# A message-passing graph layer on one core: single-row fetches four a step on two queues, edge loads one group at a time, and the pipeline's lags taken in at the fiftieth group from the end

## The chip, the core and the metric

The kernel runs on one core of a Trainium2 chip. Its engines are TensorE (PE; its weight loads are shown apart as PEld), VectorE (DVE), ScalarE (ACT), GpSimd (POOL) and SyncE (SP). SP computes nothing here: it loads registers and issues transfers. ACT and POOL issue transfers too, beside their other work. The metric is the device time of one execution in microseconds (us), lower is better.

## What is computed

The reference is one layer of a graph network over 12,500 nodes of 64 features and 200,000 edges, sorted by destination node, followed by a residual and a layer norm. Shortened to what matters (`ssp` is softplus minus ln 2):

```python
nodes = x[[src, dst]]                            # 200000 x 128, gathered rows
gates = ssp(edge_state @ We1 + be1) @ We2 + be2
gates = gates * (1 - sigmoid(5 * (distance - 3.5)))
h = ssp(nodes @ Wn1 + bn1) @ Wn2 + bn2
messages = h * gates
message_sum = zeros.at[dst].add(messages)        # scatter-add
new_state = x + (ssp(message_sum @ Ws1 + bs1) @ Ws2 + bs2)
out = layernorm(x + new_state)
```

## The kernel before, in words

**Tiling.** The edges are cut into 391 groups of 512 (`NG`), each held as four slots (`K = 4`) of 128 edges. The rows of `x` for an edge's source must be fetched one by one. The destination side needs no gather: a table of `x @ Wn1` (lower half) is made in a preparation of about 75 us, and since edges are sorted, the destinations of 256 edges lie within 42 consecutive nodes (`W`), so `load` (line 231) brings a strip of 42 table rows per half group.

**How source rows come.** A slot is normally filled by one indirect gather on POOL (`gather`, line 193, issued in line 205): 128 rows of 256 bytes, indices in `src_i`. Some slots are instead filled row by row with ordinary 256-byte transfers by SP's and ACT's queues (`fetch`, line 209, issued in line 225 after the row numbers were put in registers by the load of line 218). SP fills 14 slots at 5 rows a step, ACT 17 slots at 6 rows a step (`SYNC_ROWS`, `SCALAR_ROWS`, `slots_by_rows`, line 102); these slots lie in tiles `xr`, the gathered ones in `xg`. 18 `xg` buffers exist (`AHEAD + BEHIND`), and a gather is issued 14 groups ahead.

**A step.** The main loop (line 592) runs over steps `i`. Its order is written out by hand and the engines keep it. In a step before `ends = 390 - CATCH_UP`, SP issues the loads of group `i+5` (line 236 the edge features `eT`, in even steps for two groups at once; line 240 loads registers; line 245 twice the table strip `wns`), then its rows. PE does for different groups: the edge half of the second layer of group `i-1` (lines 303, 307), the first layer of group `i+1` (270, 272, 278), the scatter by a one-hot matrix of group `i-3` (330), the transposes of group `i+3` (261) and the node half of the second layer of `i-1` (313). ACT does the exponential of group `i+1` (line 289), two single rows, the logarithm (292), two rows, the copy of the transposed rows of `i+3` (266) and two rows. DVE does the softplus' last part (297), products (322, 326), the sum into `sums` (347) and the one-hots of group `i+5` (251). So three lags stand between the transposes of a group, its first layer, its second layer and its scatter.

**Waits that order the queues.** The loads of group `g` are kept behind the scatter of group `g - 11` (`old`, line 232). The first instruction of PE's step (line 303) takes the waits of the step upon itself: the loads of the group, and the gather and the one-hots of the group to be transposed (`needs`, line 600).

**The end.** From step `ends` on, another branch (line 631) is run, in which the lags shrink: second layer lag 1 to 0, scatter lag 3 to 1, transposes from `i+3` to `i+1`; the order on PE is transposes, first layer, second layer, scatter. `CATCH_UP = 10` makes this 10 steps from the last group.

**Node blocks.** Whenever 512 more nodes are complete, their output is made by a chain of parts (`node_block`, line 349) strewn over the following steps: 25 blocks, whose PE work is in lines 366, 394 and 397, with one load and one store on SP each.

The lines that set the rates of rows and the order within a step:

```python
fetch(i, nc.sync)
...
at(exps, i + 1)
fetch(i, nc.scalar, 0, 3)
at(logs, i + 1)
fetch(i, nc.scalar, 1, 3)
for g in ahead[i]:
    transposes(g)
    xcopy(g)
fetch(i, nc.scalar, 2, 3)
```

Of the kernel before, what the change touches and what calls it, by code (L numbers as in the profile page):

```python
# [32 lines left out]

# [3 lines left out]

# [5 lines left out]
F32 = mybir.dt.float32  # L43
BF16 = mybir.dt.bfloat16
I32 = mybir.dt.int32
# [11 lines left out]
P = 128  # L57
D = 64
HE = 256
# [6 lines left out]
AHEAD = 14  # L66
LOADS = 5
SPREADS = 5
CATCH_UP = 10
PREPARE = 5  # L70
FREE = 5
BEHIND = 4


BLOCK_STEPS = ((2, 3, 4, 4, 6, 7, 8, 9, 10, 14), (2, 3, 3, 4, 5, 6, 7, 8, 9, 10), (1, 2, 1, 2, 3))
SYNC_ROWS = 5
SCALAR_ROWS = 6
CUTOFF = 5.0
EPS = 1e-5
LN2 = 0.6931471805599453  # L80
# [18 lines left out]
    return steps  # L99


def slots_by_rows(NG, k, rows):

    ready = [-(-(n + 1) * P // rows) + 6 for n in range(NG)]
    return [(g, k) for g in ready if g < NG - 2]


@with_exitstack
def gnn_resnorm_kernel(ctx: ExitStack, tc: tile.TileContext, a: dict, out: bass.AP, E: int):
# [63 lines left out]
    def note(key, ins):  # L173
        made.setdefault(key, []).append(ins)
        return ins

    def behind(ins, *keys):

        for key in keys:
            for other in made.get(key, []):  # L180
                tc.add_manual_dep(ins.ins, other.ins.name,
                                  mybir.DependencyInfo(mybir.DependencyClass.Sync, mybir.DependencyReason.DATA),
                                  reason="one place of a step takes its waits")

    lists, by_rows = {}, []
    for engine, name, k, rows in ((nc.sync, "rows_sync", K - 1, SYNC_ROWS), (nc.scalar, "rows_scalar", K - 2, SCALAR_ROWS)):
        lists[engine] = rows, slots_by_rows(NG, k, rows), const.tile(a[name].shape, I32, name=name)
        by_rows += lists[engine][1]

    def padding(g, k):  # L190
        return g * GE + k % 2 * HE + k // 2 * P >= E
# [14 lines left out]
                out=xg[:, k, :D], out_offset=None, in_=x,  # L206
                in_offset=bass.IndirectOffsetOnAxis(ap=src_i[:, g, k : k + 1], axis=0)))

    def fetch(i, engine, part=0, parts=1):

        rows, slots, rows_i = lists[engine]
        at = i * rows
        total = min(rows, len(slots) * P - at)
        if i < 0 or total <= 0:
            return
        if part == 0:
            n, first = divmod(at, rows_i.shape[1])
            _, row_at[engine] = nc.values_load_multi_w_load_instructions(  # L218
                rows_i[n : n + 1, first : first + total], engines=[engine.engine], min_val=0, max_val=N - 1,
                skip_runtime_bounds_check_because="src holds rows of x")  # L220
        for j in range(part * rows // parts, min(total, (part + 1) * rows // parts)):
            n, r = divmod(at + j, P)
            if r == 0:
                xrs[slots[n]] = loads.tile([P, P], F32, name=f"xr{slots[n][1]}", bufs=2)
            note(("gather", slots[n][0]), engine.dma_start(xrs[slots[n]][r : r + 1, :D],  # L225
                                                           x[bass.ds(row_at[engine][j], 1), :]))

    row_at = {}
    bases = {}

    def load(g):
        old = ("scatter", g - LOADS - 2 - 4)
        if g % 2 == 0:
            n = min(2, NG - g)
            both = loads.tile([P, 2, HE], F32, name="eT", bufs=4)
            behind(note(("load", g), nc.sync.dma_start(both[:, :n], a["eT"][:, g : g + n, :])), old)
            for j in range(n):
                eTs[g + j] = both[:, j]
        if g % 2 == 0:
            _, at = nc.values_load_multi_w_load_instructions(  # L240
                base_i[0:1, 2 * g : 2 * g + 4], engines=[SP], min_val=0, max_val=N - 1,
                skip_runtime_bounds_check_because="they were clamped to these bounds")
            bases[g], bases[g + 1] = at[:2], at[2:]
        for h in range(2):
            behind(note(("load", g), nc.sync.dma_start(wns[D:DW, g % REST, h, :], table[bass.ds(bases[g][h], W), :])),  # L245
                   old)
# [39 lines left out]
    def exps(g, part=every):  # L286
        if part.start == 0:
            us[g] = work.tile([P, 3 * HE], F32, name="u")
        nc.scalar.activation(us[g][:, part], z_of(g)[:, part], AF.Exp)  # L289
# [147 lines left out]
    with tc.manual_schedule():  # L437
# [4 lines left out]
        with tc.tile_pool(name="prep", bufs=1) as prep:  # L442
# [10 lines left out]

            for i in range(3):
                load_x(i)
            nc.sync.dma_start(lists[nc.sync][2], a["rows_sync"])
            nc.sync.dma_start(lists[nc.scalar][2], a["rows_scalar"])
            dist = cut.rearrange("p g k -> p (g k)")
            nc.sync.dma_start(dist, a["dist_l"])
            dst_i = rel.bitcast(I32)  # L460
# [106 lines left out]
        with tc.tile_pool(name="finish", bufs=1) as finish:  # L567
# [24 lines left out]
            for i in range(-3, last - 1):  # L592
                now = parts.pop(i, [])
                early = [part for part in now if part.tensor]
                at(load, i + LOADS)
                fetch(i, nc.sync)
                if i >= 0:
                    at(gather, i + AHEAD, i < BEHIND)
                if i < ends:
                    needs = [("xcopy", i + 1), ("load", i + 1)]  # L600
                    needs += [(name, g) for g in ahead[i] for name in ("gather", "onehot")]
                    for g in second[i]:
                        layer2_edge(g, *needs)
                    if i >= -1:
                        zs[i + 1] = z_tile()
                        layer1_edge(i + 1)
                        for part in early:
                            part.tensor(tx_tile())
                    if i >= -1:
                        layer1_node(i + 1)  # L610
                    for n, g in enumerate(third[i]):
                        scatter(g, zs[i + 1][:, 1, HE + 2 * W * n : HE + 2 * W * (n + 1)])
                    at(exps, i + 1)
                    fetch(i, nc.scalar, 0, 3)
                    at(logs, i + 1)
                    fetch(i, nc.scalar, 1, 3)
                    for g in ahead[i]:
                        transposes(g)
                        xcopy(g)
                    fetch(i, nc.scalar, 2, 3)  # L620
                    for g in second[i]:
                        layer2_node(g)
                    for g in second[i]:
                        hcut(g)
                        message(g)
                    for g in third[i]:
                        window(g)
                    for part in early:
                        part.others()
                    at(softplus, i + 1)  # L630
                else:
# [3 lines that stand above are left out]
                    zs[i + 1] = z_tile()  # L635
                    layer1_edge(i + 1)
                    for part in early:
                        part.tensor(zs[i + 1][:, 1, HE:])
                    layer1_node(i + 1)
                    exps(i + 1)  # L640
                    logs(i + 1)
                    for g in second[i]:
                        layer2(g)
                        hcut(g)
                        message(g)
                    softplus(i + 1)
                    for g in third[i]:
                        scatter(g, tx_tile()[:, : 2 * W])
                        window(g)
                    for part in early:  # L650
                        part.others()
                for g in ahead[i]:
                    at(onehot, g + 2)
                for part in now:
                    if not part.tensor:
                        part.others()
                complete = third[i][-1] + 1 if third[i] else 0
                if blocks and complete >= blocks[0][1] - PREPARE and not begun:
                    begun = node_block(*blocks[0][0], finish)
                    begun.pop(0).others()  # L660
                if blocks and complete >= blocks[0][1]:
                    steps = next(steps for steps in BLOCK_STEPS if i + steps[-1] < last - 1)
                    for n, part in zip(steps, begun):
                        parts.setdefault(i + n, []).append(part)
                    rest = begun[len(steps) :]
                    blocks.pop(0)
                    begun = None
# [119 lines left out]
def layouts(inputs):  # L787
# [18 lines left out]

    out = {"x": np.ascontiguousarray(x)}
    out["src_l"] = lanes(src, 0)
    for name, k, rows in (("rows_sync", K - 1, SYNC_ROWS), ("rows_scalar", K - 2, SCALAR_ROWS)):
        v = out["src_l"].reshape(P, NG, K)[(slice(None), *zip(*slots_by_rows(NG, k, rows)))].T.reshape(-1)  # L810
        n = lcm(P, rows)
        out[name] = padded(v, -(-v.shape[0] // n) * n, 0).reshape(-1, n)
    out["dst_l"] = lanes(dst, dst[-1])
    out["dist_l"] = lanes(dist, 1e6)
    out["dst_h"] = np.ascontiguousarray(padded(dst, NR * P * HE, dst[-1]).reshape(NR, P, HE).transpose(1, 0, 2))
# [42 lines left out]
```

## Time and profile before

| | |
|---|---|
| Time, median of 3 runs | 2429.64 us (2419.54 to 2435.27) |
| Time of the profiled execution | 2429.64 us |
| Span of the profiled execution, first to last instruction | 2427.7 us |
| Granted TensorE clock, mean over the span | 0.870 |
| Busy: PE, PEld | 2099.0 us (86%), 1723.6 us (71%) |
| Busy: POOL, DVE, ACT | 1453.4 us (60%), 1068.8 us (44%), 941.2 us (39%) |
| Mean rate of the DMA engines | 59 GB/s |

The profile is one execution as the hardware profiler saw it, on a page with several views: busy time by engine, the span in 40 slices, the queues, the chain of work that ended last (followed back from the last instruction, at each step to what released it), the costliest groups of instructions by source line, and the issued transfers. Engine names with a q (SPq, ACTq) are the engine's instruction queue, which issues transfers and loads registers; that is not counted as busy. In a line of the view of waits stand the engine and line that waited, what ended the wait, the total in us, how often, and the longest. A busy PE is not PE at full speed: when the granted clock is low its instructions take longer.

### The profile page before, as it was taken

Reading aid. Unit: us, or ns where it says so; the run is one execution under the profiler, and the core shown is the slowest. Engines: PE = TensorE matmul, PEld = TensorE weight load, DVE = VectorE, ACT = ScalarE, POOL = GpSimd, SP = SyncE. Lnnn points to the kernel's source line nnn. Section 1 sums busy time; section 2 is a strip of 40 time slices with the busy share of each in tenths; the row PEclk is TensorE's granted clock in tenths of the full one; section 3 lists DMA queues with packets and bytes.
Section 4 is the critical chain, followed back from the end, with each engine's and each line's share of the span. In section 5 each row is a group of like instructions: output and inputs, shape, how many; then the busy total and the mean of one; then the engine's idle time right before and its main releaser. Section 6 shows DMA issues by size and latency. Waiting matters only on the chain.

```text
span 2427.7 us, 48622 instructions
## 1 busy us (share of the span) xinstructions
PE 2099.0 (86%) x11373; PEld 1723.6 (71%) x11373; DVE 1068.8 (44%) x2763; ACT 941.2 (39%) x1318; POOL 1453.4 (60%) x1536
## 2 busy tenths in 40 slices
PE   5889888888788888988888888888988888888997
PEld 5777776766667676776777777777777777777775
DVE  4344333433344344343434444444444444444564
ACT  1334333433334334333434334444444444443453
POOL 6767555655657556555656656666566666665630
PEclk9989777987899779688878888999899898898997
DMA  7322212221222122122222222222222222222220
GB/s 226 102 60 61 50 45 50 55 51 43 53 51 62 46 48 58 43 53 53 58 48 57 51 55 57 56 63 59 54 60 60 57 57 59 56 64 54 60 61 8
DMA packets 147206, 143.55 MB, mean 59 GB/s; under 512 B 47912, under 2 KB 94426, under 8 KB 146916
## 3 DMA queue, kind: packets, MB, share of 16 engines
q1 hardware_dynamic: 92172, 88.01, 12.8%
q0 software_dynamic: 49024, 50.30, 10.7%
q10 hardware_dynamic: 5720, 2.07, 0.4%
q8 instruction: 97, 1.59, 0.3%
q14 instruction: 193, 1.58, 0.2%
HBM read 130.58 MB, written 9.63 MB: 58 GB/s over the span
## 4 chain that ended last, share of the span: by engine, by line
PE 46%; SPq 21%; DMA 10%; issue 10%; ACTq 7%; ACT 5%; DVE 1%; DVEq 0%
PE z L278 11%; SPq L218 7%; PE z L272 7%; PE gh L307 7%; DMA xr<-in_x 6%; ACTq L225 5%; SPq L245 5%; PE z L330 5%; PE gh L313 5%; SPq L225 4%; PE gh L303 3%; ACT xT L266 3%; PE tx L261 3%; DMA wns<-table 3%; SPq L240 3%
## 5 line engine op out<-in xcount | busy, mean ns | idle before, releaser
L205 POOL DMA_INDIRECT xg<-in_x,src_i x1532 | 1453.2, 949 | 883.3 <-PE z L330 398.5
L297 DVE SCALAR_TENSOR_TENSOR s<-u,z 128x768 f32<-128x768 f32 x392 | 372.9, 951 | 709.0 <-ACT u L292 698.8
L292 ACT ACTIVATE u<-u,one 128x768 f32<-128x768 f32 x392 | 365.9, 934 | 781.0 <-DMA xr<-in_x 771.1
L278 PE MATMUL z<-xT,wns 106*128 106x256 f32 x1564 | 494.2, 447 | 0.0
L289 ACT ACTIVATE u<-z 128x768 f32<-128x768 f32 x392 | 316.3, 807 | 398.1 <-PE z L330 122.1
L313 PE MATMUL gh<-consts,s 128*128 128x64 f32 x3128 | 423.9, 282 | 0.0
L313 PEld LDWEIGHTS gh<-consts,s 128*128 128x128 f32 x3128 | 419.0, 208 | 0.0
L278 PEld LDWEIGHTS z<-xT,wns 106*128 106x128 f32 x1564 | 351.2, 226 | 64.0 <-ACT xT L266 0.7
L303 PE MATMUL gh<-row,ones 3*128 3x512 bf16 x391 | 157.5, 403 | 258.2 <-ACT xT L266 232.7
L322 DVE TENSOR_TENSOR h<-gh,cut 128x256 f32<-128x256 f32 x391 | 164.8, 421 | 347.2 <-PE gh L313 340.5
L272 PE MATMUL z<-eT,consts 128*128 128x256 f32 x782 | 314.7, 488 | 0.0
L307 PE MATMUL gh<-consts,s 128*128 128x128 f32 x1564 | 307.3, 324 | 0.0
L330 PEld LDWEIGHTS z<-xg,msg 128*128 128x128 f32 x1512 | 277.8, 229 | 33.3
L266 ACT COPY xT<-tx 106x512 f32<-106x512 f32 x391 | 225.2, 576 | 186.6 <-DMA xr<-in_x 134.6
L307 PEld LDWEIGHTS gh<-consts,s 128*128 128x128 f32 x1564 | 226.0, 208 | 99.5 <-issue 98.9
L261 PE MATMUL tx<-consts,xg 128*106 128x128 f32 x1533 | 272.9, 306 | 27.3 <-ACT xT L266 23.2
L330 PE MATMUL z<-xg,msg 128*128 128x84 f32 x1512 | 256.3, 300 | 0.0
L347 DVE TENSOR_TENSOR sums<-sums,z 64x42 f32 x756 | 148.7, 197 | 234.0 <-ACT u L289 159.9
L303 PEld LDWEIGHTS <-ones 3*128 3x128 bf16 x391 | 35.7, 91 | 298.2 <-ACT xT L266 258.9
L261 PEld LDWEIGHTS tx<-consts,xg 128*106 128x106 f32 x1533 | 210.6, 161 | 31.9 <-ACT xT L266 26.7
L326 DVE TENSOR_TENSOR msg<-gh,h 128x256 f32<-128x256 f32 x391 | 166.0, 424 | 13.4
L272 PEld LDWEIGHTS z<-eT,consts 128*128 128x128 f32 x782 | 131.9, 212 | 54.1 <-issue 15.4
(101 smaller groups left out, 716.7 us busy)
## 6 DMA issues: line engine op xcount, KB each, us to landing
eT<-in_eT SPq DMA_DIRECT2D x195, 256.0 KB
xr<-in_x ACTq DMA_DIRECT2D x2176, 0.2 KB
xr<-in_x SPq DMA_DIRECT2D x1792, 0.2 KB
xg<-in_x,src_i POOLq DMA_INDIRECT x1532
wns<-table SPq DMA_DIRECT2D x782, 21.0 KB
table<-tb SPq DMA_DIRECT2D x14, 448.0 KB
sums<-in_xT SPq DMA_DIRECT2D x7, 455.0 KB
y<-in_x SPq DMA_DIRECT2D x24, 128.0 KB
```

What stands on the lines that cost most here:

```text
L205: note(("gather", g), nc.gpsimd.indirect_dma_start(out=xg[:, k, :D], out_offset=None, in_=x, in_offset=bass.IndirectOffsetOnAxis(ap=src_i[ ...
L261: nc.tensor.transpose(tx[:, k, :], row, ident)
L266: note(("xcopy", g), nc.scalar.copy(xT, xTs[g]))
L272: nc.tensor.matmul(zs[g][:, 0, :HE], we1.rearrange("a h d -> a (h d)"), eTs[g], start=False, stop=True, skip_group_check=True)
L278: nc.tensor.matmul(zn, wns[:, g % REST, h, :], xTs[g][:, h], start=True, stop=True, skip_group_check=True)
L289: nc.scalar.activation(us[g][:, part], z_of(g)[:, part], AF.Exp)
L292: nc.scalar.activation(us[g][:, part], us[g][:, part], AF.Ln, bias=one)
L297: nc.vector.scalar_tensor_tensor(ss[g].rearrange("p i t e -> p (i t e)")[:, part], us[g][:, part], BIG, z_of(g)[:, part], OP.min, OP.max)
L303: first = nc.tensor.matmul(gh, ones3[:, :P], row3.rearrange("q i k d -> q (i k d)"), start=True, stop=False, skip_group_check=True)
L307: nc.tensor.matmul(v[:, 0, t], ss[g][:, 0, t, :], we2, start=False, stop=False, skip_group_check=True)
L313: nc.tensor.matmul(ghs[g][:, 1, 2 * t + h, :], ss[g][:, 1 + h, t, :], wn2, start=False, stop=h == 1 and t == 1, skip_group_check=True)
L330: ins = nc.tensor.matmul(sc, msgs[g][:, 2 * t : 2 * t + 2, :].rearrange("p h f -> p (h f)"), xgs[g][:, 2 * t : 2 * t + 2, D:DW], start=t = ...
```

## The change

Two settings are changed together, with the code that goes with them.

- Rows: SP and ACT fetch four rows a step each (`ROWS`) instead of five and six. Each fills 12 slots instead of 14 and 17, and both fill slots of the same groups (every 32nd from 36 on). ACT's four rows stand two behind the exponential and two behind the logarithm; the two behind the copy of the transposed rows are gone. The row numbers lie in one table with a slot's 128 numbers in one partition, loaded four at a time. POOL gathers 1539 slots instead of 1532. Rows are fetched up to step 383, instead of 358 (SP) and 362 (ACT).
- Edge features: `eT` is loaded for one group in every step instead of two groups in every second step: 391 transfers of 128 KB instead of 195 of 256 KB and one of 128 KB, into seven buffers of one group instead of four of two.
- `CATCH_UP` is 50 instead of 10: the branch with short lags runs from step 340 instead of 380, and gets ACT's row fetches, since rows are still fetched there.

```diff
-CATCH_UP = 10
+CATCH_UP = 50
...
-SYNC_ROWS = 5
-SCALAR_ROWS = 6
+ROWS = 4
...
-def slots_by_rows(NG, k, rows):
-
-    ready = [-(-(n + 1) * P // rows) + 6 for n in range(NG)]
-    return [(g, k) for g in ready if g < NG - 2]
+def slots_by_rows(NG):
+
+    return [(g, k) for k in (K - 1, K - 2) for g in range(P // ROWS + 4, NG - 2, P // ROWS)]
...
-    def fetch(i, engine, part=0, parts=1):
-
-        rows, slots, rows_i = lists[engine]
-        at = i * rows
-        total = min(rows, len(slots) * P - at)
-        if i < 0 or total <= 0:
+    def fetch(i, engine, first=0, count=ROWS):
+
+        n, r = divmod(i * ROWS + first, P)
+        if i < 0 or n >= len(by_rows) // 2:
             return
-        if part == 0:
-            n, first = divmod(at, rows_i.shape[1])
+        n += half_of[engine]
+        if r == 0:
+            xrs[by_rows[n]] = loads.tile([P, P], F32, name=f"xr{by_rows[n][1]}", bufs=2)
+        if first == 0:
             _, row_at[engine] = nc.values_load_multi_w_load_instructions(
-                rows_i[n : n + 1, first : first + total], engines=[engine.engine], min_val=0, max_val=N - 1,
+                rows_i[n : n + 1, r : r + ROWS], engines=[engine.engine], min_val=0, max_val=N - 1,
                 skip_runtime_bounds_check_because="src holds rows of x")
-        for j in range(part * rows // parts, min(total, (part + 1) * rows // parts)):
-            n, r = divmod(at + j, P)
-            if r == 0:
-                xrs[slots[n]] = loads.tile([P, P], F32, name=f"xr{slots[n][1]}", bufs=2)
-            note(("gather", slots[n][0]), engine.dma_start(xrs[slots[n]][r : r + 1, :D],
-                                                           x[bass.ds(row_at[engine][j], 1), :]))
+        for j in range(count):
+            note(("gather", by_rows[n][0]), engine.dma_start(xrs[by_rows[n]][r + j : r + j + 1, :D],
+                                                             x[bass.ds(row_at[engine][first + j], 1), :]))
...
     def load(g):
+        eTs[g] = loads.tile([P, HE], F32, name="eT")
         old = ("scatter", g - LOADS - 2 - 4)
-        if g % 2 == 0:
-            n = min(2, NG - g)
-            both = loads.tile([P, 2, HE], F32, name="eT", bufs=4)
-            behind(note(("load", g), nc.sync.dma_start(both[:, :n], a["eT"][:, g : g + n, :])), old)
-            for j in range(n):
-                eTs[g + j] = both[:, j]
+        behind(note(("load", g), nc.sync.dma_start(eTs[g], a["eT"][:, g, :])), old)
...
                     at(exps, i + 1)
-                    fetch(i, nc.scalar, 0, 3)
+                    fetch(i, nc.scalar, 0, ROWS // 2)
                     at(logs, i + 1)
-                    fetch(i, nc.scalar, 1, 3)
+                    fetch(i, nc.scalar, ROWS // 2, ROWS // 2)
                     for g in ahead[i]:
                         transposes(g)
                         xcopy(g)
-                    fetch(i, nc.scalar, 2, 3)
...
                     layer1_node(i + 1)
                     exps(i + 1)
+                    fetch(i, nc.scalar, 0, ROWS // 2)
                     logs(i + 1)
+                    fetch(i, nc.scalar, ROWS // 2, ROWS // 2)
```

More of the change, by code (lines that the diff above doesn't have):

```diff
@@ L35 @@
 from contextlib import ExitStack
-from math import ceil, lcm, sqrt
+from math import ceil, sqrt
 import concourse.bass as bass
@@ L183, in behind @@
                                   reason="one place of a step takes its waits")
[L185 to L188, printed above, removed]
+    by_rows = slots_by_rows(NG)
+    rows_i = const.tile([len(by_rows), P], I32, name="rows_i")
+    half_of = {nc.sync: 0, nc.scalar: len(by_rows) // 2}
     def padding(g, k):
@@ L455, in gnn_resnorm_kernel @@
                 load_x(i)
-            nc.sync.dma_start(lists[nc.sync][2], a["rows_sync"])
-            nc.sync.dma_start(lists[nc.scalar][2], a["rows_scalar"])
+            nc.sync.dma_start(rows_i, a["rows"])
             dist = cut.rearrange("p g k -> p (g k)")
@@ L808, in layouts @@
     out["src_l"] = lanes(src, 0)
[L809 to L812, printed above, removed]
+    out["rows"] = np.ascontiguousarray(out["src_l"].reshape(P, NG, K)[(slice(None), *zip(*slots_by_rows(NG)))].T)
     out["dst_l"] = lanes(dst, dst[-1])
```

## The prediction

> **What bounds the kernel now.** I read the page first, then the waits, one stretch of the chain, and the engines' work by stretch.
>
> ```profile
> PE 2099.0 (86%) x11373; PEld 1723.6 (71%) x11373; DVE 1068.8 (44%) x2763; ACT 941.2 (39%) x1318; POOL 1453.4 (60%) x1536
> PE 46%; SPq 21%; DMA 10%; issue 10%; ACTq 7%; ACT 5%; DVE 1%; DVEq 0%
> L205 POOL DMA_INDIRECT xg<-in_x,src_i x1532 | 1453.2, 949 | 883.3 <-PE z L330 398.5
> ```
>
> PE looks like the bound with 86%, but it holds less than half of the chain; 38% of it are queues and transfers (SPq, DMA, ACTq).
>
> ```profile
> ACT u L292 <- DMA xr<-in_x: 771.1, 360, 5.5
> POOL xg L205 <- PE z L330: 398.5, 190, 6.3
> POOL xg L205 <- issue: 369.2, 1207, 0.6
> PE gh L303 <- ACT xT L266: 232.7, 163, 2.9
> ACT xT L266 <- DMA xr<-in_x: 134.6, 107, 4.2
> ACT u L289 <- DMA xr<-in_x: 120.3, 96, 5.2
> ```
>
> ACT stands 1026 us (771.1 + 134.6 + 120.3) behind its own single-row transfers, 2.6 us a step, and PE then waits for ACT. POOL in turn waits for PE. The chain shows why a row takes so long to be issued:
>
> ```profile
> 1501.00 0.42 PE z L330 x4
> 1501.44 0.36 SPq L236
> 1503.79 1.33 SPq L218
> 1508.35 1.32 SPq L218
> 1510.72 1.48 DMA xr<-in_x
> 1512.22 0.22 ACTq L225
> 1512.48 0.60 ACT xT L266
> 1513.59 0.37 PE gh L303
> ```
>
> A scatter on PE lets SP start; SP works two steps through (9 us, of which 2.65 load registers); one of its rows lands 1.48 us later; only then does ACT issue a row, copy, and let PE go on. ACT waits for SP's row because the transfers of both queues share eight semaphores, and each waits for the one before it on the same semaphore. The list of the built program's instructions shows the waits, for ACT:
>
> ```
> L289 Activation u<-z 128x768 [waits DVE_49,PE_49]
> L218 TensorLoad rows_scalar
> L225 DMACopy xr<-in_x 1x64 [waits DMAHW1_49]
> L225 DMACopy xr<-in_x 1x64 [waits DMAHW2_49]
> L292 Activation u<-u,one 128x768 [waits Activation_49]
> ```
>
> Traced back by the semaphores' values, ACT's rows 2 to 5 of step 200 wait for SP's rows 1, 3, 4 and 5 of step 203. From step 36 on it is so all along: several of ACT's six rows wait for SP's transfers 3 to 5 steps further on. But SP's step 203 is kept behind the scatter of group 197, which PE does in step 200. So within every step: scatter, then SP's work, then ACT, then PE.
>
> Without rows the loop is gone, which the last stretches show (busy us and counts of PE, PEld, DVE, ACT, POOL; granted clock; DMA):
>
> ```profile
> 360.00:1200.00 840.00, 717.00 (x3810) 588.04 (x3808) 339.71 (x872) 310.32 (x428) 498.13 (x527) 0.84 0.22 51
> 2270.00:2340.00 70.00, 70.00 (x439) 57.98 (x438) 43.90 (x116) 37.32 (x57) 48.24 (x51) 0.98 0.28 67
> ```
>
> In the timeline ACT's exponentials start 6.02 us apart with rows (78.2 to 2198.2 us, 352 steps), and 4.35 apart after the last row (2318.68, 2323.03, 2327.38), with PE gapless at clock 0.98. About 0.9 us of the 1.67 between them is the lower clock (0.84 against 0.98 on some 5 us of work), which comes with the gaps, and 0.1 the blocks.
>
> **The change part by part.**
>
> *Order of the transfers.* With 4 + 4 rows and one `eT` a step, 11 transfers a step (13.5 before) go over the eight semaphores, and the built program deals them out differently: up to step 345 ACT's rows wait for SP's transfers of the step before or the same step (one ahead at most), SP's for ACT's of the same or the step before. The wait for work three steps ahead, behind this step's scatter, is gone, and with it the loop. In steps 0 to 3 of before, where SP is not yet needed ahead, exponentials are 3.57 to 4.29 us apart although ACT issues six rows in each: ACT's own issuing isn't the bound. So the step falls to PE's 4.35, or to the next thing. At steps 345 to 354 the required lead of SP grows by three steps; at 3.9 us of SP work each that is up to 11 us of waiting, once.
>
> *Register loads.*
>
> ```profile
> L218 ACTq TENSOR_LOAD <-rows_scalar x363: 506/1150/1755, 81.8 to 2268.0; - x182
> L218 SPq TENSOR_LOAD <-rows_sync x359: 697/1327/1497, 83.9 to 2225.8; - x180
> L240 SPq TENSOR_LOAD <-base_i x196: 482/497/958, 72.2 to 2359.0; - x196
> ```
>
> Durations are least, median, most, in ns. Line 240 loads four aligned numbers in 0.50 us, and ACT's last load, of four, is the 0.506. So the new loads cost 0.5: 0.83 less on SP, 0.65 less on ACT.
>
> *SP's queue a step*, pieces of the chain with their gaps: `eT` 0.41 (before every second step), line 240 0.56 (every second), two strips 1.0, load 1.38, rows 0.41 each. Before 0.21 + 0.28 + 1.0 + 1.38 + 2.05 = 4.9; after 0.41 + 0.28 + 1.0 + 0.55 + 1.65 = 3.9, hidden beside PE's 4.35. Uncovered, the 195 extra `eT` issues would be 80 us.
> [...] The trace pays 0.37 us of queue for one, and the waits for `eT` are 17.1 us before line 289 and 9.3 before line 385 in all.
>
> *ACT.* Two rows (0.4 each) less between copy and exponential; 3.3 us a step at most (2.3 of instructions, the load and rows partly under them), hidden.
>
> *POOL is late next.* A gather takes 0.944 and 0.306 of issue behind it, 1.25 us, back to back from 2270 to 2340. A full group of four is 5.0 us, more than PE's 4.35. By 100 us 71 are started; 1539 - 71 = 1468 x 1.25 = 1835 us, so the last ends at 1935. Its start is 11 groups ahead of PE's transposes; at 0.4 us a step this lead lasts some 130 steps, then PE goes at POOL's rate. From the last transposes to the end before takes 28.6 us (2399.1 to 2427.7); landing of a gather has no row, the nearest is a row's 1.48 to 1.75, I take 1.7. Sum 1935 + 1.7 + 28.6 = 1965, with the 1.9 outside the span 1967.
>
> *PE alone* would need 78 + 391 x 4.35 + 24 blocks x 2 steps x 1.0 (steps with a block's matmuls are 5.2 to 5.4) + 25 = 1852, below POOL.
>
> *CATCH_UP.* Steps of the short branch are 4.41 to 4.51 us apart on PE (line 278 at 2370.57, 2375.08; 2382.38, 2386.79): 0.1 x 40 = 4 us, under POOL's rate. Two steps there with a block's work took 7.2 and 7.36, 3.9 more than two such steps before; for five more blocks 0 (other list of steps, more distance between parts; POOL covers 0.5 us a step) to 19 us. I take 10. The rows of ACT in this branch stand before the copy that PE needs at once: 0 (it was not shown waiting) to 1.3 us a step.
> The clock: PE waits that remain are POOL's 0.4 to 0.6 us a step; in the trace stretches with waits up to 2.9 us at line 303 have 0.84, the last without them 0.98. I take 0.95 or more.
> [...]
>
> Sum: 1967 + 11 + 10 = **1988**. The profiled execution is the median run (2429.64), so no shift is needed. Faster or slower by under 1% counts as the same.
>
> **Rivals.**
> - *B, the loop stays* in other shape (ACT still waits for SP behind the scatter). For it: the lead of two to four steps from step 348 on. Against: before that there is none. Then only its pieces shrink: in the stretch shown (four steps), two loads by 0.83 and a row 0.42 less, an `eT` 0.41 more, 1.67, so 0.42 a step; 343 x 0.42 = 144, **2285**.
> - *C, no change*: ACT's waits only mirror slack and something else paces the steps at 6.02: **2430**. Against: the 4.35 as soon as rows end.
> - *D, slower*: SP and ACT in lockstep, so that ACT's rows each wait a fresh landing instead of an old one. ACT's 3.3 plus two landings of 1.65 is 6.6 a step: 78 + 384 x 6.6 + 30 = **2640**. It decides from 0.7 us of wait a row ((6.02 - 3.3)/4); before it was 0.47 (1026/2176). Against: in the new order a landing has most of a step's time. The short branch could do it too, at the 8.1 us of its slowest step: 44 x 2.1 = 92 us, if the other steps gained under 0.27.
>
> **How the numbers follow.** Forecast (POOL paces) 0.72, B 0.15, C 0.03, D 0.10. Forecast's own range: 1945 (the last 28.6 us ran at half clock for most; at full some 10 less, and neither 11 nor 10 paid) to 2070 (0.55 us of waits left in each of PE's 391 steps on 1856). The range goes to B and a little over, 1945 to 2330; outside stay D and tails. Faster 0.87, same 0.03, slower 0.10.
>
> **What would show it.** Right: ACT's waits for row transfers under 150 us in all; POOL's wait for PE's scatter under 60; PE's line 303 waiting for gathers; register loads of 0.5; clock over 0.93. Wrong: ACT still over 1.5 us a step behind rows, or steps from 340 over 5.5 us apart.

## The result, and the profile after

| | before | after |
|---|---|---|
| Time, median of 4 runs | 2427.32 us (2419.54 to 2435.27) | 2034.15 us (2023.74 to 2059.65) |
| Time and span of the profiled execution | 2429.64 us, 2427.7 us | 2023.74 us, 2022.0 us |
| Granted TensorE clock | 0.870 | 0.969 |
| Stretches at half clock, their sum | 98, 635 us | 16, 129 us |
| A step, mean of steps 36 to 340 | 6.10 us | 4.85 us |
| A step, mean of steps 340 to 380 | 5.33 us | 5.94 us |
| Last gather of POOL starts | 2336.0 us | 1940.1 us |

The ratio is 0.8366, 95% interval 0.8319 to 0.8413; the slowest run after (2059.65 us, granted clock 0.948 where the others have 0.959 to 0.969) is left out of it as a slow run. The prediction was 1988.0 us, 2.3% too low. (A step is the distance of two exponentials of ACT over whole groups. The half-clock stretches are summed from the trace's own record of the granted clock.)

The page of the changed kernel: busy time, the shares of the chain that ended last, and POOL's gathers.

```profile
PE 1867.1 (92%) x11373; PEld 1531.4 (76%) x11373; DVE 1079.0 (53%) x2756; ACT 928.4 (46%) x1318; POOL 1463.7 (72%) x1543
...
PE 72%; SPq 8%; DMA 8%; issue 5%; DVE 3%; ACT 3%; ACTq 1%; DVEq 0%
...
L202 POOL DMA_INDIRECT xg<-in_x,src_i x1539 | 1463.5, 951 | 477.0 <-issue 339.1
```

PE does the same 11373 matmuls in 232 us less busy time, with a granted clock of 0.969 instead of 0.870. Queues and transfers (SPq, DMA, ACTq) had 38% of the chain and have 17%. POOL's gathers now stand idle mainly for their own issue.

The waits of the changed kernel. Its lines lie ten or so above those of before: 282 is the logarithm (292), 279 the exponential (289), 256 the copy of xT (266), 202 the gather (205), 293 the start of the second layer (303), 303 its node half (313), 268 the first layer (278), 320 the scatter (330). Dots stand for lines left out.

```profile
POOL xg L202 <- issue: 339.1, 1112, 0.3
ACT u L282 <- DMA xr<-in_x: 296.7, 371, 1.1
...
PE gh L293 <- DMA xr<-in_x: 43.1, 68, 1.1
...
POOL xg L202 <- PE z L320: 34.7, 114, 0.3
...
PE z L268 <- ACT xT L256: 10.2, 14, 1.6
...
ACT xT L256 <- DMA xr<-in_x: 6.4, 10, 1.4
```

ACT's 1026 us behind its own rows have become 303, and the longest is 1.4 us instead of 5.5. What is left is 0.8 us in each of 371 steps, as much as the issue of the two rows that stand in front of the logarithm takes (0.41 us each), and PE waits little for it. POOL's 398 us behind PE's scatter have become 35.

The engines' work by stretch (us, busy time and count of PE, PEld, DVE, ACT, POOL; granted clock; DMA share; GB/s):

```profile
360.00:1200.00 840.00, 780.83 (x4901) 649.10 (x4900) 450.87 (x1138) 395.91 (x555) 635.96 (x670) 0.99 0.28 66
1200.00:1780.00 580.00, 542.82 (x3321) 444.97 (x3321) 318.99 (x824) 271.88 (x396) 438.77 (x464) 0.97 0.29 68
1780.00:1850.00 70.00, 66.60 (x340) 49.15 (x339) 31.73 (x85) 29.14 (x43) 52.94 (x56) 0.83 0.26 61
1850.00:1950.00 100.00, 93.68 (x499) 68.73 (x499) 48.08 (x131) 42.77 (x62) 69.04 (x73) 0.88 0.25 61
```

From 360 to 1200 us POOL does 670 gathers where it did 527, one each 1.254 us: it is back to back, and the clock is 0.99 instead of 0.84. The last two stretches lie in the branch with short lags, which now begins at step 340, at 1712 us. There the clock drops to 0.83, and POOL, whose gathers had been about 4.5 groups ahead of ACT's exponentials since step 100, is 10 groups ahead again at step 360. In this stretch it is not POOL that paces.

The loads of row numbers (least, median, most in ns):

```profile
L215 ACTq TENSOR_LOAD <-rows_i x384: 483/490/527, 80.8 to 1971.0; - x192
L215 SPq TENSOR_LOAD <-rows_i x384: 467/562/782, 85.4 to 1956.0; - x192
```

They took 1.15 and 1.33 us before.

What happens in the short branch, in the timeline of ACT at its first node block (start us, us):

```profile
1749.35 0.94 ACT L282 ACTIVATE u<-u,one 128x768 f32<-128x768 f32 x1 [0.78 <-DMA xr<-in_x]
1750.65 0.61 ACTq L219 DMA_DIRECT2D xr<-in_x  x2
1751.31 0.42 ACT L375 ACTIVATE l_s<-l_s 128x256 f32<-128x256 f32 x1 [1.02 <-DMA xr<-in_x]
1751.76 0.51 ACT L376 ACTIVATE l_s<-l_s,half 128x256 f32<-128x256 f32 x1
1752.17 0.56 ACT L256 COPY xT<-tx 106x512 f32<-106x512 f32 x1
```

And of PE over the same time and behind it:

```profile
1748.52 1.00 PE L303 MATMUL gh<-consts,s 128*128 128x64 f32 x8
...
1752.79 1.13 PE L268 MATMUL z<-xT,wns 106*128 106x256 f32 x4 [1.53 <-ACT xT L256]
...
1754.72 1.81 PE L303 MATMUL gh<-consts,s 128*128 128x64 f32 x8
...
1772.61 1.81 PE L303 MATMUL gh<-consts,s 128*128 128x64 f32 x8
...
1779.83 1.00 PE L303 MATMUL gh<-consts,s 128*128 128x64 f32 x8
```

ACT's copy of xT stands behind two rows, and behind two activations of the node block of which the first had to wait for the rows to be issued. In the short branch PE needs the copy at once, and waits 1.53 us for it. Soon after that one wait PE's matmuls take 1.81 us instead of 1.00 for 24 us, although PE has no gap in that time. The clock's record has three such stretches in the branch, at 1755, 1806 and 1905 us, each of 23.9 us. They follow the waits for the copy at the first, second and fourth of the four blocks between steps 340 and 380 (1.53, 1.57 and 1.40 us); at the third the wait was 0.97 us, and the clock stayed. Steps in the stretches take 7.5 to 9.7 us.

### The profile page after: what moved, and what is told of

Read it like the earlier page. It is cut to its first block, busy times and chain, and to the rows that moved or that the text cites. A ratio compares the mean times of both kernels' runs of the same rounds, so it can differ in the third digit from the quotient of the medians.

```text
span 2022.0 us, 46191 instructions
## 1 busy us (share of the span) xinstructions
PE 1867.1 (92%) x11373; PEld 1531.4 (76%) x11373; DVE 1079.0 (53%) x2756; ACT 928.4 (46%) x1318; POOL 1463.7 (72%) x1543
## 3 DMA queue, kind: packets, MB, share of 16 engines
q8 instruction: 96, 1.57, 0.3%
## 4 chain that ended last, share of the span: by engine, by line
PE 72%; SPq 8%; DMA 8%; issue 5%; DVE 3%; ACT 3%; ACTq 1%; DVEq 0%
PE z L268 15%; PE gh L303 11%; PE gh L297 10%; PE z L262 10%; DMA xr<-in_x 6%; PE z L320 6%; PE tx L251 6%; PE gh L293 5%; PE z L260 3%; SPq L235 3%; SPq L219 2%; SPq L215 2%; ACT u L279 2%; PE z L530 2%; DVE h L312 1%
## 5 line engine op out<-in xcount | busy, mean ns | idle before, releaser
L268 PE MATMUL z<-xT,wns 106*128 106x256 f32 x1564 | 422.4, 393 | 10.3 <-ACT xT L256 10.2
L303 PE MATMUL gh<-consts,s 128*128 128x64 f32 x3128 | 400.8, 272 | 0.0
L303 PEld LDWEIGHTS gh<-consts,s 128*128 128x128 f32 x3128 | 389.4, 196 | 0.1
L268 PEld LDWEIGHTS z<-xT,wns 106*128 106x128 f32 x1564 | 302.8, 196 | 63.6 <-ACT xT L256 20.1
L297 PE MATMUL gh<-consts,s 128*128 128x128 f32 x1564 | 282.1, 303 | 0.0
L262 PE MATMUL z<-eT,consts 128*128 128x256 f32 x782 | 281.4, 442 | 0.0
L297 PEld LDWEIGHTS gh<-consts,s 128*128 128x128 f32 x1564 | 206.7, 192 | 92.3 <-issue 90.3
L251 PE MATMUL tx<-consts,xg 128*106 128x128 f32 x1540 | 239.8, 279 | 4.0 <-DVE xg L241 2.7
L320 PEld LDWEIGHTS z<-xg,msg 128*128 128x128 f32 x1352 | 210.0, 196 | 19.3
L320 PE MATMUL z<-xg,msg 128*128 128x84 f32 x1352 | 198.1, 269 | 0.0
L251 PEld LDWEIGHTS tx<-consts,xg 128*106 128x106 f32 x1540 | 184.8, 145 | 5.1 <-DVE xg L241 3.0
```

The lines of the kernel that those rows point to most:

```text
L251: nc.tensor.transpose(tx[:, k, :], row, ident)
L262: nc.tensor.matmul(zs[g][:, 0, :HE], we1.rearrange("a h d -> a (h d)"), eTs[g], start=False, stop=True, skip_group_check=True)
L268: nc.tensor.matmul(zn, wns[:, g % REST, h, :], xTs[g][:, h], start=True, stop=True, skip_group_check=True)
L297: nc.tensor.matmul(v[:, 0, t], ss[g][:, 0, t, :], we2, start=False, stop=False, skip_group_check=True)
L303: nc.tensor.matmul(ghs[g][:, 1, 2 * t + h, :], ss[g][:, 1 + h, t, :], wn2, start=False, stop=h == 1 and t == 1, skip_group_check=True)
L320: ins = nc.tensor.matmul(sc, msgs[g][:, 2 * t : 2 * t + 2, :].rearrange("p h f -> p (h f)"), xgs[g][:, 2 * t : 2 * t + 2, D:DW], start=t = ...
```

## The experiments

There were twelve experiments, in three sets of four; those of a set shared one chip and the runs of the kernel before on it. Two kernels stand in both of the first two sets. The third set's chip ran the kernel before in 2425 us, as in the result above. The chips of the first two ran it in 2856 and 2826 us, so ratios of those sets are not comparable with the others. In their traces some of SP's instructions are stretched, and 60 to 70% of the semaphore events that the other traces hold are missing. The changed kernel itself, on the chip of the second set (least, median, most in ns):

```profile
L219 ACTq FUSED_REGOPS  x1536: 37/37/42, 92.1 to 2550.8; - x192
...
L219 SPq FUSED_REGOPS  x1536: 2/37/1400, 97.6 to 2535.7; - x192
```

In the profiled run of the result above the second line reads

```profile
L219 SPq FUSED_REGOPS  x1536: 37/37/42, 86.0 to 1957.9; - x192
```

The same register operation, which waits for nothing, is recorded with up to 1.4 us on SP there (144 of the 1536 with over 0.3 us) and 0.04 on ACT. Sets 1 and 2 therefore show the kernels on chips where, by the record, SP is slow; I call it the slow SP below. How slow it is can't be read from its times: 148 of the packets of SP's rows start up to 1.2 us before the recorded start of the instruction that issues them, where on the first chip none starts less than 0.84 us after it. The longer times of the runs stand. What slows them is open.

| Set | Kernel | Median us | Ratio to before, 95% interval |
|---|---|---|---|
| 1 | changed, tenth group | 2595.8 | 0.9147 (0.9087 to 0.9207) |
| 1 | before, fiftieth group | 2893.52 | 1.018 (1.0067 to 1.0292) |
| 1 | before, SP 5 rows, ACT 4 | 2861.26 | 1.0046 (1.0003 to 1.0088) |
| 1 | before, SP 4 rows, ACT 6 | 2751.53 | 0.9687 (0.9591 to 0.9783) |
| 2 | changed, as it is | 2604.23 | 0.9216 (0.9138 to 0.9294) |
| 2 | changed, tenth group | 2558.07 | 0.9076 (0.8997 to 0.9155) |
| 2 | before, SP 5 rows, ACT 4 | 2802.97 | 0.993 (0.9891 to 0.9969) |
| 2 | before, loads let go one group earlier | 2791.58 | 0.9865 (0.9772 to 0.9959) |
| 3 | before, no single rows | 2021.31 | 0.8347 (0.8295 to 0.8399) |
| 3 | before, SP's rows only | 2071.33 | 0.8549 (0.8493 to 0.8606) |
| 3 | before, 4 and 4 rows | 1990.8 | 0.8223 (0.8173 to 0.8274) |
| 3 | changed, no single rows | 2018.21 | 0.8322 (0.8262 to 0.8382) |

And from the profiled executions, in us (steps 36 to 340, steps 340 to 380, start of the last gather, span):

| Kernel | 36 to 340 | 340 to 380 | last gather | span |
|---|---|---|---|---|
| before | 6.10 | 5.33 | 2336.0 | 2427.7 |
| changed | 4.85 | 5.94 | 1940.1 | 2022.0 |
| set 3, before, 4 and 4 rows | 4.88 | 4.99 | 1945.6 | 1996.5 |
| set 3, before, no rows | 4.95 | 5.04 | 1974.0 | 2020.4 |
| set 3, changed, no rows | 4.96 | 5.32 | 1971.4 | 2023.5 |
| set 3, before, SP's rows only | 5.08 | 4.99 | 1978.7 | 2070.1 |
| set 2, changed | 6.28 | 7.33 | 2496.6 | 2601.8 |
| set 2, changed, tenth group | 6.26 | 6.11 | 2450.1 | 2550.1 |

### The parts by themselves (set 1)

The change has three parts: the rows, the edge loads and `CATCH_UP`. The changed kernel with the third put back:

```diff
-CATCH_UP = 50
+CATCH_UP = 10
```

> The changed kernel with CATCH_UP back at 10, so that only the rows and the edge loads differ from the kernel before. Theory (the gain is the order of the row transfers, POOL paces from about step 85 on, and the 50 steps of the short branch cost some 50 us): last gather near 1935 us, 30 us behind it, 1965 to 1985 us, no step of 9 us before step 380. Rival (the longer short branch is itself part of the gain): not under 2034 us, more likely near 2100 or above.

The kernel before with that setting alone, and ACT's row fetches in the short branch:

```diff
-CATCH_UP = 10
+CATCH_UP = 50
...
                     exps(i + 1)
+                    fetch(i, nc.scalar, 0, 3)
                     logs(i + 1)
+                    fetch(i, nc.scalar, 1, 3)
+                    fetch(i, nc.scalar, 2, 3)
```

> The kernel before with CATCH_UP at 50 alone; ACT's rows are fetched in the short branch too, two behind the exponential and four behind the logarithm. Theory: steps to 340 stay at about 6.0 us, ACT's waits for row transfers stay over 850 us, the short branch is no faster than the steps it replaces: 2400 to 2470 us. Rival (the short branch brings the gain): under 2150 us.

The kernel before with other numbers of rows, one of which turns the order of the dealing round and one leaves it:

```diff
-SCALAR_ROWS = 6
+SCALAR_ROWS = 4
```

> The kernel before with four rows a step for ACT and five for SP as before, edge loads in pairs and CATCH_UP 10 as before. In the built program ACT's rows wait for SP's transfers 2 to 4 steps back instead of 3 to 5 ahead, while SP's queue keeps its five rows and its 1.33 us register loads. Theory (order): the loop is gone though SP is as heavy as before (4.9 us a step, about POOL's rate): 1980 to 2070 us. Rival (weight: SP's queue work of 4.9 us a step sets the loop's length): two rows less on ACT save at most 0.8 us a step, 2130 to 2300 us.

```diff
-SYNC_ROWS = 5
+SYNC_ROWS = 4
```

> The kernel before with four rows a step for SP (register loads of four, about 0.5 us) and six for ACT as before. In the built program ACT's rows still wait for SP's transfers three steps ahead. Theory (order): the loop stays and only its pieces shrink, 0.83 and 0.42 us a step at SP, of which 0.4 to 0.6 us a step show: 2200 to 2310 us, ACT's waits for rows over 700 us. Rival (weight): SP at 3.7 us a step is out of the way, 1980 to 2080 us.

Measured: 0.9147, 1.018, 1.0046 and 0.9687. As shares of 2427 us my theories had 0.81 to 0.82, 0.99 to 1.02, 0.82 to 0.85 and 0.91 to 0.95; only the second was met, at its edge. As these chips are slower from the start, the first and the last are weak tests. The gain lies with the rows and edge loads and not with the fiftieth group, which costs. That five and four rows gain nothing speaks against my theory as I had put it: ACT's rows there follow SP's of 2 to 4 steps earlier, but SP's rows then wait for ACT's of two steps later (564 of the 1520 in steps 36 to 340, by the semaphores in the trace), which I had left out. The profile of its repeat in set 2 has the loop the other way round: ACT waits little for rows (30 us in place of 1026), and PE waits for the strips that SP loads late.

```profile
ACT u L289 <- PE z L330: 837.0, 175, 9.8
...
PE gh L303 <- DMA wns<-table: 276.4, 119, 8.8
```

The times were some 18% above those of the first profile, so the next set had the changed kernel itself in it.

### The changed kernel on such a chip, and a later gate (set 2)

> The changed kernel as it is, beside its variants on one chip. In the first runs of this study (another chip) a variant whose first 340 steps are issued in the same order took 6.2 us a step all the way, with the TensorE clock halving every few steps, where the changed kernel had 4.35 to 4.9 us. Theory: the long steps belonged to that chip and not to the variant; then this run is within 2% of the ratio 0.837 if SP's register operations take 0.04 us again, or at 0.90 to 0.93 if they take some tenths of a us as on the other chip. Rival: the variant's later branch changed the early steps; then this run has 0.837 on any chip.

> The changed kernel with the lags taken in at the tenth group from the end again, the rows dealt as the change deals them. Theory: the short branch of steps 340 to 380 cost the changed kernel 42 to 58 us (a late copy of xT behind ScalarE's rows and the block's logarithms, then 24 us at half clock, three times), so this one takes 0.97 to 0.985 of the changed kernel's time on the same chip. Rival: those steps are long for another reason (the block's own work), and the time stays within 1% of the changed kernel's.

> The kernel before with one number changed: ScalarE's queue fetches four rows a step and not six, SyncE's five as before; pairs of edge loads, lags and helpers as before. ScalarE's rows then wait for SyncE's of 2 to 4 steps earlier, not 3 to 5 steps later. Theory (the order on the shared semaphores is the loop): ScalarE's waits for its own rows fall below 400 us and the ratio to the kernel before is 0.82 to 0.87. Rival (the single edge loads, the cheaper row-number loads and the short branch are what gained): the ratio is 0.95 to 1.00.

```diff
-    REST = LOADS + 2
+    REST = LOADS + 3
...
-        old = ("scatter", g - LOADS - 2 - 4)
+        old = ("scatter", g - LOADS - 3 - 4)
...
-            both = loads.tile([P, 2, HE], F32, name="eT", bufs=4)
+            both = loads.tile([P, 2, HE], F32, name="eT", bufs=5)
```

> The kernel before with SyncE's loads kept behind the scatter of one group earlier and one buffer more for the edge loads and the node weights: SyncE may run one group further ahead. ScalarE's rows still wait for SyncE's of about four steps later. Theory (the order moves with the loads, the loop stays closed whatever the gate's depth): ratio 0.98 to 1.02. Rival (the depth of the gate is what holds SyncE and through it ScalarE): ratio 0.90 to 0.95.

Measured: 0.9216, 0.9076, 0.993 and 0.9865. The first lies in the theory's 0.90 to 0.93: the changed kernel is as long-stepped there as its variant, so the 6.2 us belong to the chips and not to the variant. The third, a repeat, lies in the rival's range and not in the theory's; its reason is the loop turned round, as above, and the rival's single edge loads and short branch are ruled out as the gain by set 3.

Measurements from the traces tell the two conditions apart. By the records, the issue of a row waits for the same one of eight semaphores that its own transfer raises: all 2176 of ACT's rows and 1790 of SP's 1792 in the kernel before, all 1536 and 1535 of 1536 in the changed one. I took each row of ACT whose semaphore was last used by a row of SP. In steps 36 to 340 of the kernel before, SP's row is nearly always one of three steps later (956 of 959); in the changed kernel it is one of the step before or of the same step (557 of 557). The time from that row's data packet to the end of ACT's issue has a median of 0.93 us in the kernel before, 4.10 us in the changed one, 4.30 in the kernel before with four and four rows, and 0.86 us in the changed kernel with the slow SP; the least is about 0.55 in the first, second and last. And ACT stands idle in front of the issue of a row (gaps over 0.15 us) for 485 us in all in the kernel before, 15 in the changed one, 1 with four and four rows, and 306 in the changed kernel with the slow SP. So before, more than half of these rows were issued within 1 us of the packet of SP's row; after the change the landing is long past; and with a slow SP the same order puts ACT right behind SP again, as in the lockstep of rival D. The working of D gave 2640 us, the run 2604, but how much of the run's length comes from that lockstep and how much from the slow SP itself is not shown.

The tenth group instead of the fiftieth saves 46 us here (2604.23 to 2558.07, a factor of 0.982), as expected: steps 340 to 380 fall from 7.33 to 6.11 us. The gate's depth matters little: 0.9865 lies in the theory's range, and the rival's 0.90 to 0.95 is out.

### The rows taken away, and dealt evenly (set 3)

The kernel before without single rows; then with SP's rows only:

```diff
-        lists[engine] = rows, slots_by_rows(NG, k, rows), const.tile(a[name].shape, I32, name=name)
+        lists[engine] = rows, [], const.tile(a[name].shape, I32, name=name)
```

> The kernel before without any fetch of single rows: GpSimd gathers those 31 slots too (1563 gathers instead of 1532), all else as before. Theory (the rows on the two queues hold the steps, through their shared semaphores): no step is longer than GpSimd's four gathers of 1.25 us, the last gather ends at about 1970 us, the run at about 2000 us, ratio 0.70 to 0.73, clock above 0.93. Rival (SyncE's slow instructions, or clock halving that keeps itself up, hold the steps here, rows or not): ratio 0.90 or more.

```diff
+        slots = slots_by_rows(NG, k, rows) if engine is nc.sync else []
-        lists[engine] = rows, slots_by_rows(NG, k, rows), const.tile(a[name].shape, I32, name=name)
+        lists[engine] = rows, slots, const.tile(a[name].shape, I32, name=name)
```

> The kernel before with SyncE's five rows a step alone; ScalarE fetches none and GpSimd gathers its 17 slots. Nothing of ScalarE's can wait for a transfer. Theory (what costs is that ScalarE's rows stand in front of its logarithm and its copy): ratio 0.71 to 0.80. Rival (the number of rows on SyncE, whose loads come late, is what costs): ratio 0.92 to 1.00.

The kernel before with nothing but two numbers changed:

```diff
-SYNC_ROWS = 5
-SCALAR_ROWS = 6
+SYNC_ROWS = 4
+SCALAR_ROWS = 4
```

> The kernel before with four rows a step on each queue, pairs of edge loads, its own helpers and the tenth group. Both queues then wait for each other's transfers of -2 to +1 steps, as in the changed kernel. Theory (the order of the dealing decides): the ratio is that of the changed kernel with the tenth group here, 0.89 to 0.93. Rival (the single edge loads or the aligned row numbers make the gain): 0.96 to 1.00.

The changed kernel without single rows:

```diff
-    half_of = {nc.sync: 0, nc.scalar: len(by_rows) // 2}
+    by_rows = []
+    half_of = {nc.sync: 0, nc.scalar: 0}
```

> The changed kernel (fiftieth group, single edge loads) without any fetch of single rows. Theory for the short branch (the copy of xT comes late because ScalarE's rows and the block's logarithms stand in front of it): without the rows steps 340 to 380 stay under 5.2 us and the time is within 1% of the kernel before without rows. Rival (the branch itself, its order or the block's work, costs): these steps stay 1 us or more longer than in the kernel before without rows, 30 to 50 us in all, 1.5 to 2.5% slower than that one.

Measured: 0.8347, 0.8549, 0.8223 and 0.8322. The ratios that I gave for the first three came from wrong bases, 2800 us for the first two and the slow SP's 0.908 for the third, and all three were missed. For the first the time is what counts: about 2000 expected and 2021 measured without rows, with steps of 4.95 us, near four gathers of 1.25 us. The second's 0.71 to 0.80 of 2800 us is 1988 to 2240 us, and 2071 were measured.

Without any row the kernel before is as fast as the changed one. So the rows, which spare POOL 31 of 1563 gathers or 39 us, cost 404 us more than they saved, some 440 in all. Take away ACT's alone and 354 of these 404 us are gone; the rest goes with SP, which with five rows a step is itself the pace. The chain of that kernel says so (line numbers of this kernel are one higher, the load is line 219):

```profile
PE 45%; SPq 31%; issue 11%; DMA 5%; POOL 4%; DVE 2%; ACT 1%; DVEq 0%; POOLq 0%
```

```profile
L219 SPq TENSOR_LOAD <-rows_sync x359: 693/1329/1502, 83.8 to 1897.7; - x180
```

Its steps are 5.08 us with POOL 11 to 14 groups ahead of ACT's exponentials; the working of SP's queue in the prediction had 4.9.

The third kernel is the clear one. Two numbers make the whole gain and 43 us more than the change (1990.8 against 2034.15, each with the kernel before at 2425 to 2427 us). This rules out its rival, that the single edge loads make the gain; the cheaper row-number loads (0.48 us on ACT and 0.56 on SP) are in it too. Its waits:

```profile
POOL xg L205 <- issue: 351.2, 1151, 0.3
...
PE gh L303 <- DMA xr<-in_x: 32.5, 50, 1.3
POOL xg L205 <- PE z L330: 28.7, 94, 0.3
...
ACT u L289 <- DMA xr<-in_x: 11.9, 5, 3.9
...
ACT u L292 <- DMA xr<-in_x: 1.3, 2, 0.7
```

ACT's waits for its rows are 13 us in place of 1026, and POOL paces at 4.88 us a step. Here SP issues one row less a step and ACT two less, each loads four aligned row numbers, and each waits for the other's transfers of two steps before to one step ahead. The run doesn't part the order from the smaller number of rows or from the cheaper loads. Set 1 does in part, with a slow SP: nine rows dealt as five and four gained nothing, ten dealt as four and six 3%, the changed kernel with eight dealt evenly 8 to 9%, so on those chips it is not the number of rows alone. Eleven rows dealt in the good order were not tried.

Without rows, the fiftieth group and the single edge loads cost nothing that can be measured (2018.21 against 2021.31). But my theory said that steps 340 to 380 would then stay under 5.2 us, and they took 5.32, the first twenty 5.85: the branch still has one stretch at half clock, of 44.4 us, after a single wait of 1.31 us in front of the transposes; PE waits nowhere in the branch for the copy. As the last gather starts no later than in the kernel before without rows (1971.4 and 1974.0 us), POOL's pace hides the stretch.

```profile
360.00:1738.00 1378.00, 1263.03 (x7848) 1047.64 (x7847) 729.25 (x1850) 635.61 (x909) 1043.67 (x1098) 0.98 0.29 65
1738.00:1952.00 214.00, 210.62 (x1177) 157.44 (x1176) 112.39 (x301) 99.73 (x143) 161.89 (x172) 0.90 0.28 66
```

The second line is the short branch of the changed kernel without rows. So of the 0.95 us by which a step there is longer than in the kernel with four and four rows (5.94 against 4.99), about 0.3 come with the branch and 0.6 with the rows in it.

## Why the prediction was right, and where not

**The loop.** Right. It named ACT's rows, kept back by SP's transfers three to five steps on, as what makes 6.02 us out of 4.35. Without ACT's rows the steps are 5.08 us, without any 4.95, with four and four dealt evenly 4.88, and in the changed kernel the landing that ACT waits for is 4.1 us old instead of 0.9. What is argued and not shown is that, with rows on both queues, the order alone opens the loop: fewer rows and cheaper row-number loads came with it in every such kernel that gained on a chip with a fast SP. (SP's rows alone, with their loads of 1.33 us, gain 354 us.) Rival B (the loop stays, 2285) and C (no change, 2430) are out.

**POOL is late next.** Right: the last gather was worked out to end at 1935 us and started at 1940.1, the steps go at its rate from step 80 to step 340, and its wait for the scatter is 34.7 us (under 60 was named). That PE's line 303 (293 now) waits for gathers has no line of its own among the waits, where a wait for several semaphores is put down to one. The records show it: in steps 110 to 330 PE stands still in front of line 293 131 times, 79 us in all, and then starts 0.78 us after a gather's data have landed (0.63 to 0.90 us in 8 of 10), where gathers land 1.25 us apart.

**Register loads.** Right in size: 0.49 and 0.56 us against 0.5. What they are worth by themselves was not tried.

**Single edge loads.** Costed at nothing. Right: with rows away, the kernel with 391 single loads is no slower than the one with 195 pairs (2018.21 and 2021.31 us).

**ACT's waits for rows under 150 us.** Wrong as a sign: 303 us. It was meant to show that the loop is gone, but two rows issued in front of the logarithm are 0.8 us of wait in any step, 300 us in all. The kernel with four and four rows, which puts one there, has 13. The other sign of being wrong came too: steps 340 to 380 are 5.94 us apart, over the 5.5 that were named; that is the next point.

**CATCH_UP.** This is the step that failed. The working gave 10 us for the blocks, 11 for SP's growing lead, and 0 for ACT's rows in front of the copy, out of bounds of 0 to 1.3 us a step, because nothing had been seen waiting there. From the last gather to the end it so had 51 us (1.7 + 28.6 + 10 + 11); the run took 82, the changed kernel without rows 52 and the one with four and four rows 51. So the term put at nothing is what was missing. The rows in front of the copy cost about 0.6 us a step, inside the prediction's bounds, but not by their own length: with the block's two activations they make the copy late, and at three of four blocks PE then ran 24 us at half clock. Without rows PE never waits for the copy there, and one such stretch of 44 us is left. Set 2 measured the setting by itself, with a slow SP: 46 us. The changed kernel with the tenth group was not run on a chip with a fast SP; 43 us lie between the changed kernel and the one with four and four rows. SP's growing lead was not seen apart from this. The five more blocks that the prediction counted are four (steps 340 to 380). The other 10 us of the 46 between 1988 and 2034 are the runs' spread: the profiled execution is the fastest of the four.

**Clock.** Right: 0.969, and 0.95 or more was taken.

**Rival D.** It did not come about on the chip of the result. On chips with a slow SP ACT is right behind SP again, and the change has half of its gain (0.92 instead of 0.84). That the lockstep costs that half is not shown, since these chips differ in more than that.

## What to carry to other kernels

When two queues' transfers share semaphores, look up for each issue which earlier transfer it waits for, in the built program: here rows of ACT waited for rows that SP issues three steps later (956 of 959), and ACT stood 1026 us behind its rows, against 13 with four and four. Deal such work evenly, in the order in which both engines come to it (here four and four rows took 435 us off 2425; order, number and cheaper loads were not parted), and first ask what it saves: here the row fetches spared POOL 39 us and cost 440. Where an engine has no slack, price a late arrival with the half clock that may follow it, and not with its own length: here waits of 1.40 to 1.57 us were each followed by 23.9 us at half clock, three times, and one of 1.60 us by none.

## What the runs showed that was not expected

- A single wait of 1.4 to 1.57 us was followed by 23.9 us at half clock with PE busy throughout, three times. The length of the gap does not settle it: a wait of 1.60 us at 1679 us, in the main loop of the same run, was followed by no half clock, and one of 1.39 us in the main loop of the kernel with four and four rows by 3.4 us of it. Why the stretches in the short branch are so long is open.
- One and the same program ran steps 36 to 340 at 4.85 us on one chip (granted clock 0.969 over the run) and at 6.28 on another (0.825).
- The kernel before with two numbers changed (1990.8 us) is faster than all other kernels of this study.
